# Row maxima of a grouped attention layer: weights taken as 128 adjacent queries instead of every fourth one, and the maxima brought to the queries' rows by a transpose and on-chip transfers

## The chip, the cores and the metric

The kernel runs on one core of one Trainium2 chip. The metric is the device time in microseconds of one execution of the program; lower is better. The profile of the kernel before is one execution taken by the hardware profiler. In its lines PE is the TensorE matmul, PEld the TensorE weight load, DVE is VectorE, ACT is ScalarE, POOL is GpSimd and SP is the engine that issues most DMAs.

## The reference, cut to what matters

Four cross-attention layers run one after the other on `x` (1 x 2048 x 256) with a context of 1601 keys (512 wide). Layers 1, 3 and 4 have 16 heads of width 64 and a bias on a few columns ("masked" layers in the kernel). The second layer, which the change concerns, has 16 query heads of width 16, of which four share one key and value head ("grouped"):

```python
xn = rmsnorm(x, norm_w)
q = (xn @ wq).reshape(B, T, N_HEADS, HEAD_DIM)
k = (cond @ wk).reshape(B, S, N_KV_HEADS, HEAD_DIM)
v = (cond @ wv).reshape(B, S, N_KV_HEADS, HEAD_DIM)
qg = q.reshape(B, T, N_KV_HEADS, n_rep, HEAD_DIM)
scores = jnp.einsum('btgrd,bsgd->bgrts', qg, k) * scale
attn = jax.nn.softmax(scores.astype(jnp.float32), axis=-1).astype(q.dtype)
out = jnp.einsum('bgrts,bsgd->btgrd', attn, v).reshape(B, T, N_HEADS * HEAD_DIM)
return residual + out @ wo
```

All of it is float32. The softmax subtracts each query's maximum over the keys, so that maximum has to be known before the exponentials are taken.

## The kernel before, in words

**Units.** Work is cut into units: one group of heads and one block of 512 queries. In the grouped layer a unit is four heads that share keys and values; each head has 16 rows of a 32-row quarter of the partitions (`QUARTERS`, rows 0, 32, 64 and 96). There are 4 groups and 4 query blocks, so 16 grouped units. `self.q` holds the unit's queries, features on the partitions and 512 queries along the free dimension; `self.u.kT` holds the keys in the same way.

**Steps.** A unit goes through 13 steps, one for each chunk of 128 keys (`TCH`), the last with 65. The loop at the end runs over steps in pairs. At one step three units are at work: one is scored (`scoring`), the one before it has its exponentials taken (`exping`, 18 steps after its own scoring step), and for that one, two steps later, the values are summed (`valuing`).

**One step of the grouped layer** (`Step.grouped`) consists of two parts, each for two scoring heads and the two other heads of the unit in `exping`. A part issues to TensorE, head by head in turn:

- `row_maxima` (L718): the queries are the weights and the keys stream, so that queries come out on the partitions and keys along the free dimension. It exists only for the maximum. Each step takes 128 of the queries and 512 keys; the last step takes the 65 remaining keys for all four sets of 128 queries. VectorE reduces each result (`row_maximum`, L731; L733 for the last step) into `row_top`.
- `scores_again` (L783): the keys are the weights and the queries stream; ScalarE takes the exponentials out of PSUM (`grouped_exp`, L795).
- then `values` (L813): the weights are the values and the exponentials stream, into `po`.

While only grouped units are at work the score results take six PSUM banks (`psum.singly`); in the built program each of the two kinds of score goes round three of them. A fourth result of a kind must wait until the first has been read.

**Which queries are the weights.** The weights of L718 are `self.q[r, columns(q)]`, and `columns(q)` is every fourth query:

```python
return slice(q, QB, QT)
```

So partition p of the result holds query 4p + q, and the 4 maxima of a partition are adjacent queries.

**From the maxima to the exponentials.** When a unit's scoring ends, `maxima` reduces `row_top` to `ntop` (L754, negated; 128 partitions x 4 heads x 4). `on_all_partitions` writes it to DRAM (L655) and reads it back, one row of 512 for each head (L658), into row 16 of the head's quarter of `self.q`. Row 16 of the keys is one, so that `scores_again` yields scores less their maximum. Nothing else is done with `ntop`.

**Order.** TensorE, ScalarE and VectorE run their instructions in the written order (the manual dependencies at the end). Between the steps stand pieces (`Pieces`): projections of queries (L576), keys and values of the next block (L440, L394, L546), denominators (L843, whose weights also use `columns(q)`), output projection (L862). A piece may be given a step at which it is due (`pieces.at`). One PSUM bank, `pm` in the pool `ps_m`, serves most of these pieces in turn.

Of the kernel before, what the change touches and what calls it, by code (L numbers as in the profile page):

```python
# [10 lines left out]
FP = mybir.dt.float32  # L11
# [7 lines left out]
P = 128  # L19
# [7 lines left out]
Piece = namedtuple("Piece", "run cost shared", defaults=(True,))  # L27
# [7 lines left out]
def tile_cross_attention_stack(ctx: ExitStack, tc: tile.TileContext, t: dict, out: bass.AP):  # L35
# [31 lines left out]
    nc = tc.nc  # L67
    x, cond = t["x"], t["ctx_2048"]
# [6 lines left out]
    QT = QB // P  # L75
# [13 lines left out]
    small = ctx.enter_context(tc.tile_pool(name="small", bufs=2))  # L89
    dram = ctx.enter_context(tc.tile_pool(name="dram", bufs=1, space=bass.MemoryType.DRAM))  # L90
    ps_o = ctx.enter_context(tc.tile_pool(name="ps_o", bufs=1, space=PSUM))
    ps_m = ctx.enter_context(tc.tile_pool(name="ps_m", bufs=1, space=PSUM))
    scores_pools = ctx.enter_context(ExitStack())

    ident = const.tile([P, P], FP, name="ident")
# [267 lines left out]
    QUARTERS = (0, 32, 64, 96)  # L363
# [107 lines left out]
    class Grouped:  # L471
# [5 lines left out]
        name = "L1_xattn_"  # L477
# [166 lines left out]
    def columns(q):  # L644


        return slice(q, QB, QT)

    def on_all_partitions(cols, to):


        n = cols.shape[1]
        rows = dram.tile([4, P, QT], FP, name="cols", bufs=4)[:n]
        with nc.allow_non_contiguous_dma(reason="1024 values, four at a time"):
            nc.sync.dma_start(out=rows.rearrange("h p q -> p h q"), in_=cols)  # L655
        for tile_, heads_ in to:
            src = rows[heads_].rearrange("(o h) p q -> o (h p q)", o=1)
            nc.sync.dma_start(out=tile_, in_=src.to_broadcast(tile_.shape))  # L658


    class Unit:
# [44 lines left out]
        def row_maxima(self, i, h, s):  # L706

            full = QT * (NK - 1)  # L710
            r = self.rows(h)
            if i < full:
                q, k = divmod(i, NK - 1)
                todo = [(q, *TBK[k], 0)]
            else:
                todo = [(q, TAIL, NTAIL, q * NTAIL) for q in range(QT)]
            for q, a, n, at in todo:
                nc.tensor.matmul(  # L718
                    s[:, at : at + n], self.q[r, columns(q)], self.u.kT[r, a : a + n],
                    start=True, stop=True,  # L720
                )
                yield
# [17 lines left out]
        def maxima(self):  # L740

            ntop = small.tile([P, len(self.pair), QT], FP, name="ntop")
            if self.masked:
                pt = psum.pair((2, QT, P))
                for h in range(2):
                    for q in range(QT):
                        nc.tensor.transpose(pt[:, h, q, :], self.top[:, h, columns(q)], ident)  # L747
                nc.vector.tensor_reduce(ntop, pt, AX.X, ALU.max, negate=True)  # L748
                self.spread = work.tile([P, 2, QB], FP, name="spread", bufs=1)
                on_all_partitions(  # L750
                    ntop, [(self.spread.rearrange("n h q -> n (h q)"), slice(0, 2))]
                )
            else:
                nc.vector.tensor_reduce(ntop, self.top, AX.X, ALU.max, negate=True)  # L754
                on_all_partitions(
                    ntop,
                    [(self.q[r + 16 : r + 17, :], slice(h, h + 1)) for h, r in enumerate(QUARTERS)],
                )

        def maxima_spread(self):  # L760
# [128 lines left out]
    for b in range(NB):  # L889
        nc.scalar.dma_start(  # L890
            out=x_rows[b], in_=x[0, ts(b, QB), :].rearrange("(n p) c -> p n c", p=P)
# [47 lines left out]
    def first_unit(i):  # L939

        if i < NT / 2:
            first_block(i)
        if i == 1:
            layers[0].load_wo(made[0, 0])
            for b in range(NB):
                keep(0, b)
                pieces.at(2 * i + 2 + 2 * b, [(0, biases[b])])
        if i == 3:
            token_marks(0)
        if i == 7:  # L950
            small_constants()
            for l in range(1, NL):
                token_marks(l)
            start_block(0)
# [59 lines left out]
    pieces = Pieces()  # L1014
# [127 lines left out]
    def masked(unit):  # L1142
        return unit and unit.masked

    for first in range(0, N + NT + DELAY + LAG + 16, 2):
        pair = [Step(first), Step(first + 1)]

        if any(masked(x.scoring) for x in pair):
            if psum.banks:
                psum.by_pairs()  # L1150
        elif pair[0].exping and not pair[0].exping.masked and not psum.banks:
            psum.singly()

        kn, cn = divmod(first + 2 - NT - DELAY, NT)
        ahead = of[kn] if cn == 0 and 0 <= kn < len(units) and of[kn].masked else None
        three = not ahead and not any(masked(x.exping) for x in pair)
        for x in pair:
            x.begin()
        for x in pair:
            if masked(x.exping):  # L1160
                if x.cb == 0 and x is pair[1]:
                    x.exping.maxima_spread()
                x.exping.subtract(x.cb)
        for x in pair:
            if masked(x.scoring):
                x.scoring.masked_scores(x.ca)

        ends = all(masked(x.valuing) for x in pair) and pair[0].cv == NT - 1
        if ends:
            pair[0].valuing.values(NT - 1)  # L1170
        for x in pair:
            if masked(x.exping):
                x.exping.masked_exp(x.cb)
        if ahead:
            ahead.maxima_spread()
        if not ends:
            for x in pair:
                if masked(x.valuing):
                    x.valuing.values(x.cv)
        first_unit(first // 2)  # L1180
        together = masked(pair[0].scoring) and (masked(pair[1].exping) or not pair[1].exping)
        for x in pair:
            x.grouped(three)
            x.end()
            if not together:
                pieces.steps([x.step], x.share())
        if together:
            pieces.pair([first, first + 1], round(pair[0].units_left() * NT / 2))
        if ends:
            pair[1].valuing.values(0)  # L1190
        for x in pair:
            if x.scoring and x.ca == NT - 1:
                x.scoring.maxima()


    last = {}
# [39 lines left out]
```

## Time and profile before

| what | value |
|---|---|
| time before, median of 3 runs | 4903.22 us (4901.65 to 4903.43) |
| the profiled execution: time; span | 4898.06 us; 4896.4 us |
| TensorE clock granted, mean | 0.981 |
| busy share: PE, PEld, DVE, ACT, POOL | 97%, 42%, 77%, 66%, 61% |
| grouped scoring alone (no grouped exponentials yet) | 1295 to 1385 us |
| grouped scoring and exponentials together | 1385 to 2266 us |

The busy share of PE says only that some matmul was in flight; matmuls overlap, and so a busy PE may still lose time to weight loads. The times of matmul ends are modelled by the profiler. The stages are found in the page's row of slices (the second layer is where GpSimd has nothing to do) and in the first and last starts of L718 and L783.

### The profile page before, as it was taken

How to read it: one execution, taken by the hardware profiler on the slowest of the kernel's cores; microseconds unless marked ns; L12 is line 12 of the kernel's file. 1: busy time of each engine (PE TensorE's matmuls, PEld its weight loads, DVE VectorE, ACT ScalarE, POOL GpSimd, SP SyncE). 2: the span in 40 equal slices, each digit the busy share in tenths (PEclk: the TensorE clock that was granted, in tenths of full speed). 3: DMA queues.
4: the chain of work that ended last, by engine and by line, in shares of the span. 5: the costliest groups of instructions: out<-in, count | busy, mean ns of one | idle time of the engine just before them, and what ended most of it. 6: DMA issues, size and time to landing. Idle time of an engine off the chain costs nothing.

```text
span 4896.4 us, 64042 instructions
## 1 busy us (share of the span) xinstructions
PE 4727.9 (97%) x24004; PEld 2059.7 (42%) x24004; DVE 3746.8 (77%) x3766; ACT 3221.9 (66%) x3994; POOL 2993.3 (61%) x1440
## 2 busy tenths in 40 slices
PE   8999999999999999999999999999999999999996
PEld 4444444443444444454344444444444444444432
DVE  5888888888766565653578888888888888888886
ACT  4777777777545544544567777777777777777774
POOL 3777777778610000000377777777777777777787
PEclk9999999999989999999899999999999999999998
DMA  4222222222210000011132222222232222222201
GB/s 146 87 83 78 87 75 88 80 80 73 65 38 21 20 21 20 19 41 45 44 92 88 83 80 82 77 88 77 78 90 79 83 78 87 75 88 84 76 29 35
DMA packets 354053, 337.87 MB, mean 69 GB/s; under 512 B 120681, under 2 KB 309353, under 8 KB 353744
## 3 DMA queue, kind: packets, MB, share of 16 engines
q1 hardware_dynamic: 350048, 328.41, 22.9%
q8 instruction: 189, 3.10, 0.3%
q0 software_dynamic: 1152, 3.28, 0.2%
q10 hardware_dynamic: 2544, 2.10, 0.1%
q14 instruction: 120, 0.98, 0.1%
HBM read 318.89 MB, written 14.82 MB: 68 GB/s over the span
## 4 chain that ended last, share of the span: by engine, by line
PE 87%; DVE 10%; issue 1%; POOL 1%; ACT 1%; DMA 0%; POOLq 0%; SPq 0%; DVEq 0%; ACTq 0%
PE po L813 28%; PE s L687 19%; PE t L718 8%; PE pm L394 7%; PE pm L440 6%; PE s L862 4%; PE pm L464 4%; PE t L783 3%; DVE ntop L748 2%; DVE rden L838 2%; PE s L834 2%; DVE xs L874 2%; PE s L747 2%; DVE top L704 1%; POOL sums L778 1%
## 5 line engine op out<-in xcount | busy, mean ns | idle before, releaser
L778 POOL TENSOR_TENSOR sums<-sums,p 128x1024 f32<-128x1024 f32 (+1 forms) x1152 | 2727.9, 2368 | 739.2 <-ACT p L773 568.3
L699 ACT COPY p<-s 128x1024 f32<-128x1024 f32 (+1 forms) x1248 | 1235.4, 1014 | 663.6 <-PE s L687 578.6
L813 PE MATMUL po<-p,v 128*64 128x512 f32 (+3 forms) x8320 | 1507.3, 529 | 8.9 <-ACT p L773 5.9
L768 DVE TENSOR_TENSOR p<-p,b 128x1024 f32<-128x1024 f32 (+1 forms) x1248 | 1461.3, 1209 | 55.2 <-ACT b L763 52.9
L704 DVE TENSOR_TENSOR top<-s,top 128x1024 f32<-128x1024 f32 (+1 forms) x1056 | 1291.2, 1223 | 239.1 <-ACT p L699 175.7
L687 PE MATMUL s<-q,kT 64*128 64x512 f32 (+1 forms) x4992 | 1342.2, 631 | 86.7 <-DVE ntop L748 23.7
L773 ACT ACTIVATE p<-p 128x1024 f32<-128x1024 f32 (+1 forms) x1248 | 1254.6, 1057 | 45.7 <-DVE p L768 44.3
L813 PEld LDWEIGHTS po<-p,v 128*64 128x64 f32 (+3 forms) x8320 | 367.0, 126 | 1096.5 <-issue 864.4
L687 PEld LDWEIGHTS s<-q,kT 64*128 64x128 f32 (+1 forms) x4992 | 390.0, 182 | 725.6 <-issue 218.7
L795 ACT ACTIVATE p<-t 128x512 f32<-128x512 f32 (+1 forms) x760 | 412.2, 594 | 410.8 <-PE t L718 373.8
L731 DVE TENSOR_REDUCE row_top<-t 128x1 f32<-128x512 f32 x700 | 451.2, 686 | 256.5 <-PE t L718 253.1
L854 POOL TENSOR_TENSOR oT<-oT,by 128x512 f32<-128x512 f32 x112 | 143.3, 1280 | 758.8 <-DMA by<-cols 365.6
L718 PE MATMUL t<-kT,q 32*128 32x512 f32 (+1 forms) x1880 | 560.5, 639 | 0.0
L783 PE MATMUL t<-q,kT 32*128 32x512 f32 (+1 forms) x1520 | 491.6, 659 | 0.0
L718 PEld LDWEIGHTS t<-kT,q 32*128 32x128 f32 x1880 | 295.4, 316 | 167.6 <-issue 83.3
L394 PEld LDWEIGHTS pm<-wv,ct 128*128 128x128 f32 (+1 forms) x2600 | 300.4, 187 | 130.3 <-issue 66.9
L394 PE MATMUL pm<-wv,ct 128*128 128x128 f32 (+2 forms) x2600 | 333.3, 281 | 2.2 <-ACT v L398 0.9
L440 PE MATMUL pm<-ct,wk 128*128 128x256 f32 (+1 forms) x1344 | 314.6, 377 | 2.7 <-issue 2.7
L440 PEld LDWEIGHTS pm<-ct,wk 128*128 128x128 f32 x1344 | 230.7, 190 | 157.9 <-issue 100.1
L748 DVE TENSOR_REDUCE ntop<-s 128x8 f32<-128x1024 f32 x96 | 117.6, 1225 | 232.7 <-PE s L747 232.7
L862 PE MATMUL s<-oT,wo 128*128 128x512 f32 x392 | 199.1, 631 | 16.2 <-POOL oT L854 12.5
L776 POOL COPY sums<-p 128x1024 f32<-128x1024 f32 x96 | 99.7, 1039 | 183.6 <-ACT p L773 183.6
(149 smaller groups left out, 2308.0 us busy)
## 6 DMA issues: line engine op xcount, KB each, us to landing
ct<-ctxT SPq DMA_DIRECT2D x288, 512.0 KB
xT<-xT SPq DMA_DIRECT2D x100, 512.0 KB
spread<-cols SPq DMA_DIRECT2D x96, 512.0 KB
by<-cols SPq DMA_DIRECT2D x192, 128.0 KB
xT<-xs SPq DMA_DIRECT2D x16, 512.0 KB
ct<-ctxT SPq DMA_DIRECT2D x48, 130.0 KB
wk<-in_L_xattn_Wk_dram SPq DMA_DIRECT2D x24, 256.0 KB
wv<-in_L_xattn_Wv_dram SPq DMA_DIRECT2D x24, 256.0 KB
```

What stands on the lines that cost most here:

```text
L394: nc.tensor.matmul(pv[:md, d, :f], ct(k)[:, d * P : d * P + md], wv[:, k, :], start=(k == 0), stop=(k == NCT - 1),)
L440: nc.tensor.matmul(pk, u.wk[:, k, :], ct(k), start=(k == 0), stop=(k == NCT - 1))
L687: nc.tensor.matmul(s[:m, h, :], self.u.kT[r, a : a + m], self.q[r, :], start=True, stop=(a != TAIL),)
L699: nc.scalar.copy(p[:m], s[:m])
L704: nc.vector.tensor_tensor(self.top[:m], s[:m], self.top[:m], ALU.max)
L718: nc.tensor.matmul(s[:, at : at + n], self.q[r, columns(q)], self.u.kT[r, a : a + n], start=True, stop=True,)
L731: nc.vector.tensor_reduce(self.top[:, of, q, k : k + 1], s, AX.X, ALU.max)
L768: nc.vector.tensor_tensor(self.p[c][:m], self.p[c][:m], self.less[:m], ALU.add)
L773: nc.scalar.activation(p[:m], p[:m], AF.Exp)
L778: nc.gpsimd.tensor_tensor(self.sums[:m], self.sums[:m], p[:m], ALU.add)
L783: nc.tensor.matmul(s[:m], self.u.kT[r, a : a + m], self.q[r, :], start=True, stop=True)
L813: nc.tensor.matmul(to, v, p, start=(c == 0 and not part), stop=(c == NT - 1 and part != 0))
```

## The change

The weights of L718 become 128 adjacent queries (`ts(q, P)`). Partition p of the result then holds query 128q + p. `maxima` only reduces to `ntop`; the way through DRAM is gone for this layer. A new piece, `maxima_rows`, is due two steps after the pair of steps that ended the scoring: TensorE transposes `ntop` (128 x 16) into `pm`, ScalarE copies the 16 rows of 128 to SBUF (`top_rows`), and four DMAs from SBUF to SBUF on SP's queue put each head's 4 rows of 128 side by side into row 16 of its quarter of `self.q`. The other uses of `columns(q)` and of `on_all_partitions` stay.

```diff
-                    s[:, at : at + n], self.q[r, columns(q)], self.u.kT[r, a : a + n],
+                    s[:, at : at + n], self.q[r, ts(q, P)], self.u.kT[r, a : a + n],
...
                 nc.vector.tensor_reduce(ntop, self.top, AX.X, ALU.max, negate=True)
-                on_all_partitions(
-                    ntop,
-                    [(self.q[r + 16 : r + 17, :], slice(h, h + 1)) for h, r in enumerate(QUARTERS)],
+                self.ntop = ntop
+
+        def maxima_rows(self):
+
+            n = 4 * QT
+            pt = ps_m.tile([P, P], FP, name="pm")
+            nc.tensor.transpose(pt[:n, :], self.ntop.rearrange("p h q -> p (h q)"), ident)
+            rows = small.tile([n, P], FP, name="top_rows", bufs=1)
+            nc.scalar.copy(rows, pt[:n, :])
+            for h, r in enumerate(QUARTERS):
+                nc.sync.dma_start(
+                    out=self.q[r + 16 : r + 17, :].rearrange("o (q p) -> o q p", p=P),
+                    in_=rows[h * QT : h * QT + QT, :],
                 )
...
                 x.scoring.maxima()
+                if not x.scoring.masked:
+                    pieces.at(first + 2, [(0, Piece(x.scoring.maxima_rows, 0.3))])
```

## The prediction

> **What bounds the kernel now.** I read the page first, for the stage; then the table of windows, the groups of instructions and the waits of that stage; last the timeline of a few steps.
>
> The change touches L718 alone, which runs from 1295 to 2266 us. The windows show the stage (us; busy time of PE, PEld, DVE, ACT, POOL; granted clock; DMA):
>
> ```profile
> 1295.00:1385.00 90.00, 76.45 (x280) 30.41 (x278) 65.03 (x62) 24.86 (x26) 42.13 (x19) 0.79 0.14 44
> 1385.00:2266.00 881.00, 881.00 (x6844) 434.90 (x6840) 510.83 (x836) 436.95 (x806) 25.92 (x36) 0.97 0.10 28
> ```
>
> For 881 us PE never rests, while DVE and ACT are busy 58% and 50%. So what PE's stream of loads and passes costs is what the stage costs. The groups of that stage show both kinds of score (busy, mean ns, idle before):
>
> ```profile
> L718 PEld LDWEIGHTS t<-kT,q 32*128 32x128 f32 x1878 | 295.2, 316 | 167.6 <-issue 83.3 <-DVE row_top L731 58.2 <-DVE row_top L733 11.8
> ...
> L783 PEld LDWEIGHTS t<-q,kT 32*128 32x128 f32 (+1 forms) x1520 | 161.3, 185 | 0.1
> ...
> L843 PEld LDWEIGHTS pm<-den_rows,oT 128*128 128x128 f32 x112 | 27.2, 327 | 5.8 <-issue 5.8
> ...
> L576 PEld LDWEIGHTS pm<-xT,wq 128*128 128x128 f32 x56 | 9.5, 189 | 12.5 <-issue 12.5
> ```
>
> The same 128 columns cost 316 and 327 ns where the weights are every fourth element (L718, L843), and 185 and 189 ns where they are adjacent (L783, L576). Is the difference on the path? The timeline of one part (start, duration), with two scoring heads and two exponential heads, each in two passes:
>
> ```profile
> 1700.38 0.81 PE L718 MATMUL t<-kT,q 32*128 32x512 f32 x1
> ...
> 1700.39 0.69 PE L783 MATMUL t<-q,kT 32*128 32x512 f32 x1
> ...
> 1701.04 0.60 PE L718 MATMUL t<-kT,q 32*128 32x512 f32 x2
> ...
> 1701.57 0.64 PE L813 MATMUL po<-p,v 128*32 128x256 f32 x8
> ...
> 1701.66 1.29 DVE L731 TENSOR_REDUCE row_top<-t 128x1 f32<-128x512 f32 x2 [0.48 <-PE t L718]
> ```
>
> and, after the last scoring, a part with the exponential heads alone:
>
> ```profile
> 2271.63 1.13 PE L783 MATMUL s<-q,kT 32*128 32x512 f32 x4
> 2272.68 0.64 PE L813 MATMUL po<-p,v 128*32 128x256 f32 x8
> ```
>
> L783's second passes are done 1.13 us after the start in both (in the first, at 1701.52). L718 takes 1.26 (1700.38 to 1701.64), and the values, which need all quarters, start at 1.19 instead of 1.05. The four quarters run side by side, and the slowest chain, L718's, sets the part.
>
> [...] L783's second load of a quarter begins 108 ns after the first (2271.624, 2271.732). [...] the trace gives 233 ns from load to load (1717.863, 1718.097). [...]
>
> **The change part by part.**
>
> *Ordinary parts.* A chain is load, pass, load, pass. The second load hides under the first pass[...]; the first stands open. So each part loses 233 - 108, measured between the two chains as 1.256 - 1.134 = 0.122 us. Half the parts take 1.19 us before their values and half 1.44: there the second L718 waits until the first reduce of the part before has emptied its bank (the 58.2 us above). A part's start to start is 1.756 or 2.014, and the latter ends with the reduce: chain 1.256, start 0.03, reduce 0.69, release 0.05. The chain is a term of both, so both fall by 0.122. I count 346 such parts between 1385 and 2266: 346 x 0.122 = **42.2**. Of them 24 run at half clock[...]: **2.9**.
>
> *Last steps.* With 65 keys a head issues four queries' sets, eight loads in a row:
>
> ```profile
> 1717.43 0.30 PEld L718 LDWEIGHTS t<-kT,q 32*128 32x128 f32 x1
> ...
> 1717.63 1.74 PEld L718 LDWEIGHTS t<-kT,q 32*128 32x128 f32 x14
> ...
> 1719.44 0.16 PEld L813 LDWEIGHTS po<-p,v 128*32 128x32 f32 x8
> ```
>
> The part takes 2.02 us to its values; eight loads at 0.233 are 1.86 of it. At 0.108, and with passes in order, so that the third cannot start before L783's second at 0.55, the last of the six remaining starts at 0.55 + 5 x 0.108 = 1.09 and ends 0.21 later: 1.30, less the 0.07 by which values start early, is 1.23. If loads run freely ahead it is L783's 1.05. 30 such parts x (2.02 - 1.23) = **23.7**; bounds 18 (loads of two quarters in each other's way) and 29.
>
> *Scoring alone (1295 to 1385).* DVE is busy 65 of 90 us, PE waits for its reduces, the clock is 0.79. Twelve steps gain at most a load each at half clock, and the last step: 6. At least 0. I take **3**.
>
> *Clock.* Ten-odd stretches of 3.4 us at half clock lie in the stage; some follow the slow last steps (1722, 1780, 1896). If those three go, about 1.2 us each; **3**, between -4 (new ones behind other pieces) and 12.
>
> *Added.* 16 transposes: one pass of 128 on a 16-column load. No row shows it alone; the pieces nearest are L834, 1.17 us for eight, and L546, 0.86 on average for two longer passes. So 0.15 to 0.86, and from below slightly less than nothing, because a pause lets the reduce empty the bank (0.26). I take 0.3 on 14 of them: **-4**, range -12 to +1. Each brings an ACT copy of 16 x 128 (a 128 x 256 copy takes 0.35; ACT is half idle, and only exponentials with a spare bank are behind it) and four SP issues (0.24 each, hidden: SP issues about a dozen transfers in a unit's 57 us). `pm` is used next in a later step, after that copy.
>
> *Removed and moved.* The write of 512 pieces to DRAM and four reads go; nothing waited for them, cost and gain nothing. The order of the changed program shows a few pieces (L546 above all) a step earlier or later, none added: nothing, because PE does them anyway.
>
> *Path of the maxima.* From transpose to the first L783 that reads the row lie 6 to 8 parts of about 1.74, 10 to 14 us. Needed: transpose 0.4, copy with an exponential ahead 0.9, four issues 1.0, one landing; DRAM's was 2.3 (L655 issued 1549.65 for 0.38, L658 at 1552.33). About 4.6: hidden. Only the landing from SBUF to SBUF is not shown in the trace; it is free up to some 7.5 us.
>
> Sum: 42.2 + 2.9 + 23.7 + 3 + 3 - 4 = 70.8, of the profiled execution's 4898.06: 4827.3. The median of the runs is 5.2 above that execution; so 4832.
>
> **Rivals.**
> - *The reduces keep the pace.* If the reduce's end is not tied to the chain, only the unhindered half of the parts shrinks and the wait of the other half grows: 173 x 0.122 = 21 instead of 42, and the last steps give 18; with the other terms 21 + 1 + 18 + 3 + 3 - 4 = 42: 4861. For it: 58.2 us of waiting for L731. Against: the reduce starts 0.03 us after the chain's end in every part that I looked at, and DVE is 58% busy.
> - *Late rows, slower.* [...] an L783 that waits for its row stops L718, values, everything. It needs more than the 10 us slack plus the 70.8 gained over 16 units (4.4 each), a landing above 12 us. A landing of 14 is 6.3 late, 1.9 of net loss a unit: 16 x 1.9 = 30, 4933. Against: three times 2.3 is still free; four descriptors of 512 bytes from four partitions to one are not shown before.
> - *Loads are not what it was.* If the step did not set the load's time, no gain but the cost: 4907. Against: L843 and L576 differ in it likewise.
>
> **How the numbers follow.** Main case 0.79, reduces' pace 0.13, late rows 0.05, no effect 0.02, other 0.01. Faster by over 0.2% (10 us, about what a measurement can tell): 0.93; within: 0.02; slower: 0.05. The main case's own bounds: best 42 + 3 + 29 + 6 + 12 + 1 = 93, 4810; worst 42 + 18 - 4 - 12 = 44, 4859. The range 4812 to 4860 takes in most of it and half of the first rival.
>
> **What would show it.** L718's loads at about 185 ns; the ordinary part at 1.07 and 1.32 before its values, in about equal number; last steps near 1.23; the stage from the first joint part to 2266 some 67 us shorter; no L783 waiting for a DMA; the other stages as before. Wrong it would be with loads still near 316, with longer waits for L731, or with `q` from `top_rows` as releaser.

## The result and the profile after

The changed kernel takes **4828.29 us** (median of 4 runs, 4821.27 to 4833.60) where the kernel before, on the same chip, takes 4902.43 (4 runs, 4901.25 to 4903.43). The ratio is **0.9848, interval 0.9833 to 0.9863**: faster by 1.5%, 74.1 us. The forecast was 4832.

In the file after the change the lines below L731 stand ten lower: L793 is what L783 was (exponential scores), L805 what L795 was, L823 what L813 was, L853 what L843 was. Each kernel of the experiments has its own line numbers too; the name of the tile tells which instruction is meant.

The two stages of the second layer in the windows of the changed kernel (us; busy time of PE, PEld, DVE, ACT, POOL; granted clock, DMA share, GB/s). The windows end where the corresponding work ends, so the first number is to be compared with 90 and 881 of before:

```profile
1288.80:1378.10 89.30, 75.61 (x281) 25.99 (x279) 64.89 (x62) 24.27 (x26) 41.59 (x19) 0.75 0.14 44
1378.10:2199.90 821.80, 821.02 (x6855) 330.02 (x6854) 510.79 (x835) 440.63 (x820) 25.86 (x36) 0.97 0.11 30
```

The joint stage (scoring and exponentials together) lost some 59 us, and in it the weight loads lost 105 us of busy time (434.9 to 330.0); DVE and ACT did what they did before. PE is still all but never idle (821.02 of 821.80), so the stage is still set by PE's stream. The scoring alone did not move. Counted from the start of the first joint part to the start of the last, as from here on, the stage went from 878.9 to 820.6 us, by 58.3.

The groups of that second window (busy us, mean ns of one | idle before, and what ended it):

```profile
L731 DVE TENSOR_REDUCE row_top<-t 128x1 f32<-128x512 f32 x700 | 451.2, 686 | 215.7 <-PE t L793 186.6 <-PE t L718 29.0
...
L718 PEld LDWEIGHTS t<-kT,q 32*128 32x128 f32 x1878 | 183.5, 187 | 161.0 <-issue 94.1 <-DVE row_top L731 54.0 <-DVE xs L884 8.3
L793 PEld LDWEIGHTS t<-q,kT 32*128 32x128 f32 (+1 forms) x1520 | 163.5, 184 | 4.3 <-ACT p L805 2.5 <-issue 1.0 <-ACT rms L616 0.5
```

L718's loads went from 316 to 187 ns, level with L793; L853, whose weights are still every fourth element, stays at 327. The reduces L731 used to be released by L718 and are now mostly put down to L793. A reduce reads L718's result alone; the profile names the pass that ended last before it, so this says only that the two chains now end together: the slower chain has become as short as the other. The 14 transposes of the stage keep PE busy for 3.8 us and their copies ACT for 3.4.

One pair of ordinary parts in the timeline of the changed kernel (start, duration):

```profile
1687.17 0.69 PE L718 MATMUL t<-kT,q 32*128 32x512 f32 x1
...
1688.33 1.29 DVE L731 TENSOR_REDUCE row_top<-t 128x1 f32<-128x512 f32 x2 [0.35 <-PE t L793]
...
1688.50 0.64 PE L823 MATMUL po<-p,v 128*32 128x256 f32 x8
...
1689.07 0.69 PE L718 MATMUL t<-kT,q 32*128 32x512 f32 x1
...
1690.14 0.64 PE L823 MATMUL po<-p,v 128*32 128x256 f32 x8
```

From a part's first pass to its values (L823): 1688.50 - 1687.17 = 1.33 and 1690.14 - 1689.07 = 1.07, where it was 1.44 and 1.19. Both kinds of part fell by about 0.12.

The two parts of a last step, the first that way and the second not:

```profile
1692.60 0.32 PE L718 MATMUL t<-kT,q 32*128 32x65 f32 x1
...
1693.67 0.64 PE L823 MATMUL po<-p,v 128*32 128x256 f32 x8
1693.76 1.08 ACT L805 ACTIVATE p<-t 128x512 f32<-128x512 f32 x2 [0.77 <-PE t L793]
...
1694.24 0.32 PE L718 MATMUL t<-kT,q 32*128 32x65 f32 x1
...
1694.90 0.18 PEld L793 LDWEIGHTS t<-q,kT 32*128 32x128 f32 x1 [0.20 <-ACT p L805]
...
1695.95 0.64 PE L823 MATMUL po<-p,v 128*32 128x256 f32 x8
```

The first takes 1.07 to its values, the second 1.71. The second's L793 load stands until 1694.90, and the line says for whom: the two exponentials of the part before, which started at 1693.76 and took 1.08, so they ended at 1694.84. Before the change the first part of a last step was 2.59 us long (1717.42 to 1720.01), and those exponentials were over by then.

### The profile page after: what moved, and what is told of

Its sections match the earlier page's. It is cut to its first block, busy times and chain, and to the rows that moved or that the text cites. A ratio compares the mean times of both kernels' runs of the same rounds, so it can differ in the third digit from the quotient of the medians.

```text
span 4828.2 us, 64072 instructions
## 1 busy us (share of the span) xinstructions
PE 4667.0 (97%) x24020; PEld 1949.9 (40%) x24020; DVE 3746.8 (78%) x3766; ACT 3225.1 (67%) x4010; POOL 2991.6 (62%) x1440
## 4 chain that ended last, share of the span: by engine, by line
PE 87%; DVE 10%; issue 1%; POOL 1%; ACT 1%; DMA 0%; POOLq 0%; ACTq 0%; DVEq 0%; SPq 0%
PE po L823 28%; PE s L687 20%; PE t L718 9%; PE pm L394 7%; PE pm L440 6%; PE s L872 4%; PE pm L464 4%; DVE ntop L748 2%; DVE rden L848 2%; PE s L844 2%; DVE xs L884 2%; PE s L747 2%; DVE top L704 1%; POOL sums L788 1%; PE t L793 1%
## 5 line engine op out<-in xcount | busy, mean ns | idle before, releaser
L823 PE MATMUL po<-p,v 128*64 128x512 f32 (+3 forms) x8320 | 1506.7, 528 | 8.8 <-ACT p L783 5.8
L783 ACT ACTIVATE p<-p 128x1024 f32<-128x1024 f32 (+1 forms) x1248 | 1254.8, 1057 | 49.1 <-DVE p L778 47.7
L823 PEld LDWEIGHTS po<-p,v 128*64 128x64 f32 (+3 forms) x8320 | 366.9, 126 | 1138.9 <-issue 905.4
L805 ACT ACTIVATE p<-t 128x512 f32<-128x512 f32 (+1 forms) x760 | 413.7, 594 | 337.3 <-PE t L793 300.5
L731 DVE TENSOR_REDUCE row_top<-t 128x1 f32<-128x512 f32 x700 | 451.2, 686 | 215.7 <-PE t L793 186.6
L793 PE MATMUL t<-q,kT 32*128 32x512 f32 (+1 forms) x1520 | 496.6, 656 | 0.0
L718 PE MATMUL t<-kT,q 32*128 32x512 f32 (+1 forms) x1880 | 490.1, 563 | 0.0
L718 PEld LDWEIGHTS t<-kT,q 32*128 32x128 f32 x1880 | 183.7, 187 | 161.0 <-issue 94.1
L872 PE MATMUL s<-oT,wo 128*128 128x512 f32 x392 | 199.1, 631 | 15.1 <-POOL oT L864 11.1
```

The lines of the kernel that those rows point to most:

```text
L718: nc.tensor.matmul(s[:, at : at + n], self.q[r, ts(q, P)], self.u.kT[r, a : a + n], start=True, stop=True,)
L731: nc.vector.tensor_reduce(self.top[:, of, q, k : k + 1], s, AX.X, ALU.max)
L783: nc.scalar.activation(p[:m], p[:m], AF.Exp)
L793: nc.tensor.matmul(s[:m], self.u.kT[r, a : a + m], self.q[r, :], start=True, stop=True)
L823: nc.tensor.matmul(to, v, p, start=(c == 0 and not part), stop=(c == NT - 1 and part != 0))
```

## The experiments

Each kernel is compared with runs of the kernel before on its own chip; those medians were 4908.4 to 4910.4, 6 to 8 us above the first chip's. The times expected below start from 4828, the first chip's, and so lie as much too low; the ratios and the stages are what to compare.

**The same two kernels again**, because the profiled pair holds two things that the change does not explain: some 8 us less in the first 43 us of the program, and a stage shorter by 58 instead of 67.

> The changed kernel once more, as the base for the others on the same chip: 4828, within 4821 to 4834. Its ordinary parts with 1.07 or 1.32 us before the values, last-step parts with 1.07 (first) and 1.71 (second).

> The kernel before once more, for a second trace: its stage from the first joint part to the last 879 us as in the first trace. Where the traces of before and after differ outside that stage (7.7 us in the first 43 us), theory: that is chance of the start, and before's second trace may have it or not; rival: the change moves it.

Measured: 4835.73 for the changed kernel, ratio 0.9851 (0.9835 to 0.9868); 4910.15 for the kernel before. In the second pair of traces an early pause (PE idle for 4.4 us until 31.9 us) stands in both kernels, and both reach the first L718 at 1296.8; so the 8 us were chance. The joint stage is 885.6 before, not the 879 expected, and 820.6 after: 65.0 less. What varies is the kernel before: it spent 54.6 us of the stage at half clock in the first trace and 68.3 in the second, the changed one 44.4 in both. The pairs give the parts of the gain twice over:

| us | first pair | second pair | forecast |
|---|---|---|---|
| 346 ordinary parts | -40.4 | -45.3 | -45.1 |
| 30 last-step parts | -21.1 | -22.2 | -23.7 |
| rest of the joint stage (transposes, other pieces) | +3.2 | +2.5 | +1 |
| joint stage | -58.3 | -65.0 | -67.8 |
| scoring alone | -0.5 | -2.5 | -3 |
| start of the program, and after the last L718 | -9.4 | -5.2 | 0 |
| profiled execution | -68.2 | -72.7 | -70.8 |

The last row but one is what remains of each difference of spans: in the first pair 7.0 of it lie ahead of the first L718, in the second nothing. The other 2.4 and 5.2 fall behind the last scoring part, where nothing was forecast; they are not explained. The forecast's 3 us for the clock are counted with the rest of the joint stage.

**One half of the change at a time.** Adjacent weights, with the maxima still going through DRAM:

```diff
-                    s[:, at : at + n], self.q[r, columns(q)], self.u.kT[r, a : a + n],
+                    s[:, at : at + n], self.q[r, ts(q, P)], self.u.kT[r, a : a + n],
...
+                rows_t = dram.tile([4, QT, P], FP, name="cols_t", bufs=4)
...
+                    nc.sync.dma_start(out=rows_t.rearrange("h q p -> p h q"), in_=ntop)
...
```

> Only the weights are changed (128 adjacent queries); the maxima still go through DRAM, written in single values so that the rows come out in order; no transpose. Theory (the weight loads are all of the gain): loads of L718 near 187 ns, ordinary parts 1.07 and 1.32, and 14 transposes of 0.2 us less than the changed kernel: 4825, within 4818 to 4832. Rival (leaving DRAM brings a good part of the gain): 4850 or more. Second rival (2048 single values make the write slow, and the first exponentials of a unit wait for their row): waits of L783 for a DMA, some us a unit.

The new way for the maxima, with every fourth query as weights (so that the rows hold the maxima of other queries):

```diff
-                    s[:, at : at + n], self.q[r, ts(q, P)], self.u.kT[r, a : a + n],
+                    s[:, at : at + n], self.q[r, columns(q)], self.u.kT[r, a : a + n],
```

> Only the path is changed: transpose, copy, transfers from SBUF to SBUF; the weights stay every fourth query, so each row gets the maxima of other queries. Theory: loads of L718 near 316 ns, parts 1.19 and 1.44 as before, and 16 transposes of 0.2 us more than before: 4906, within 4902 to 4910. Rival (the path brings part of the gain): 4890 or less.

Measured: the weights alone 4837.22, ratio 0.9849 (0.9831 to 0.9867), joint stage 819.5. The path alone 4900.36, ratio 0.9993 (0.9984 to 1.0001), joint stage 881.9. The group of L718's loads in each, weights alone first, then path alone:

```profile
L718 PEld LDWEIGHTS t<-kT,q 32*128 32x128 f32 x1880 | 183.1, 188 | 166.7 <-issue 96.2 <-DVE row_top L731 56.9 <-DVE xs L878 9.9
```

```profile
L718 PEld LDWEIGHTS t<-kT,q 32*128 32x128 f32 x1880 | 295.2, 316 | 164.1 <-issue 84.4 <-DVE row_top L731 54.8 <-DVE row_top L733 11.5
```

The load's time goes with the weights' step and with nothing else, and the whole gain goes with the load's time: the weights alone are as fast as the changed kernel on the same chip (4835.73), not 3 us faster as expected, a difference too small for these runs. The transpose and the four transfers neither gain nor cost anything that they can tell: the path alone has a median 8 us below the kernel before, but its runs spread from 4894 to 4912 and those of before from 4892 to 4913, and the joint stage lies between the two of before. No exponential score waited for a row in either trace: the maxima had time enough on either way.

**Does the cost grow with the step?** If every element costs by its distance, a step of two should lie between one and four (theory B); theory A takes it to load as a step of one does.

```diff
-                    s[:, at : at + n], self.q[r, columns(q)], self.u.kT[r, a : a + n],
+                    s[:, at : at + n], self.q[r, (q // 2) * 2 * P + q % 2 : (q // 2 + 1) * 2 * P : 2], self.u.kT[r, a : a + n],
```

> The weights are every second query (step of 8 bytes), the maxima go through DRAM in pairs of values. Theory A[...]: loads from load to load 0.108 to 0.112 as with adjacent queries, and the time of weights only, 4825. Theory B (the load grows with the step, half-way between 0.108 and 0.233): loads at about 0.15, each part 0.04 longer than with adjacent queries, 4845 to 4860.

Measured: 4831.02, ratio 0.9839 (0.9822 to 0.9855), joint stage 823.2. L718's loads in the joint stage of this kernel:

```profile
L718 PEld LDWEIGHTS t<-kT,q 32*128 32x128 f32 x1878 | 190.1, 195 | 167.1 <-issue 96.5 <-DVE row_top L731 57.1 <-DVE xs L882 9.9
```

195 ns against 187 at step one and 316 at step four; in the row of loads of a last step 0.117 us from load to load, against 0.112 and 0.233. So the cost does not go with the distance: a step of two costs 8 ns more than a step of one, a step of four 129. Why four costs so much more than two is not shown; no other step was tried.

**The second part of a last step.** The reading is that its second exponential head is given the bank that the second exponential of the part before still reads. If that is the wait, two rings of three banks, one for each kind of score, should free it: there the bank is that of the first exponential, which is over half a microsecond earlier.

```diff
-            self.banks = scores_pools.enter_context(tc.tile_pool(name="ps_t", bufs=6, space=PSUM))
+            self.banks = scores_pools.enter_context(tc.tile_pool(name="ps_t", bufs=3, space=PSUM))
+            self.own = scores_pools.enter_context(tc.tile_pool(name="ps_e", bufs=3, space=PSUM))
...
-                exps = psum.heads(three) if exping else []
+                exps = psum.heads(three, True) if exping else []
```

> The changed kernel with two pools of three banks, one for the scores of the maxima and one for those of the exponentials, instead of six from one pool. Theory (in the second part of the last step the second exponential head gets a bank whose reader is the second exponential of the part before): that part falls from 1.71 to about 1.27 before its values, fifteen times 0.44: the joint stage 820.6 becomes about 814. Rival (the exponentials themselves are late): 1.71 stays.

Measured: 4828.99, ratio 0.9836 (0.9819 to 0.9854). The second parts fall from 1.71 to 1.19 or 1.26, while six of the fifteen first parts rise from 1.07 to 1.32; the 30 last-step parts go from 58.9 to 53.3 us, the stage from 820.6 to 815.0, and no L793 of the stage waits for an exponential any more. So the wait came from how the six banks are shared. Which bank it was is inferred, no trace names it; but the description ahead of the prediction, that each kind of score goes round three of the six, can't hold in the last step, or two rings of three would have changed nothing. The whole program's interval overlaps that of the changed kernel; the gain is shown in the stage alone.

**Does the reduce set the pace?** Each L731 reduces only the first half of its 512 keys, so that it is shorter:

```diff
-                nc.vector.tensor_reduce(self.top[:, of, q, k : k + 1], s, AX.X, ALU.max)
+                nc.vector.tensor_reduce(self.top[:, of, q, k : k + 1], s[:, :, : QB // 2], AX.X, ALU.max)
```

> The changed kernel with the reduce L731 over 256 of the 512 columns; the maxima are then over part of the keys. Theory A (the reduce alone makes every other ordinary part 1.32 instead of 1.07): all are 1.07, 173 x 0.25 = 43 us off the joint stage, 778. Theory B (the wait for the exponential L805 lies just behind: its end is 1.16 + 0.60 + 0.05 = 1.81 after a part's start, the next part starts at 1.64): every other part is about 1.23, 173 x 0.09 = 15 us, 805. The last steps as before in both.

Measured: 4804.05, ratio 0.9789 (0.9771 to 0.9806). The group of the reduces in the joint stage, and the windows of the two stages:

```profile
L731 DVE TENSOR_REDUCE row_top<-t 128x1 f32<-128x256 f32 x693 | 262.1, 420 | 359.5 <-PE t L793 202.2 <-PE t L718 157.3
```

```profile
1288.80:1357.70 68.90, 60.04 (x314) 26.34 (x313) 44.52 (x58) 23.68 (x28) 40.60 (x21) 0.90 0.22 60
1357.70:2168.00 810.30, 808.21 (x6789) 313.87 (x6788) 327.65 (x837) 439.18 (x814) 30.69 (x38) 0.97 0.11 30
```

A reduce shorter by 266 ns takes 183 us off DVE's joint stage and only 10.3 off the stage, near theory B (15) and far from A (43). Over a third of the ordinary parts still take 1.20 or 1.26 us to their values instead of 1.07. One of them:

```profile
1679.79 0.59 ACT L805 ACTIVATE p<-t 128x512 f32<-128x512 f32 x1
...
1680.22 0.69 PE L718 MATMUL t<-kT,q 32*128 32x512 f32 x1
...
1680.43 0.69 PE L793 MATMUL t<-q,kT 32*128 32x512 f32 x1
...
1681.49 0.64 PE L823 MATMUL po<-p,v 128*32 128x256 f32 x8
```

Its second L793 head begins 0.2 late, just behind the end of the exponential (1680.38). So the chains of loads and passes set the pace where no bank is waited for; in the other parts the reduce holds the bank, and as soon as it is shorter the exponential does. In the stage of scoring alone the shorter reduce takes 20.5 off 89.4: that stage is the reduces', which is why faster loads brought it nothing.

**Are late rows as dear as feared?** The transposes come due three steps later, so that the rows arrive near or after their first reader:

```diff
-                    pieces.at(first + 2, [(0, Piece(x.scoring.maxima_rows, 0.3))])
+                    pieces.at(first + 5, [(0, Piece(x.scoring.maxima_rows, 0.3))])
```

> The changed kernel with the transpose of the maxima due five steps after the pair that ends the scoring, not two: between it and the first exponential score that needs the row lie none or two parts instead of six or eight. Theory (the path takes about 0.6 to the first issue, 0.6 for each further one and some 2 to land, and is hidden only by the parts between): eight units wait some 2 to 4 us each, the stage grows by 16 to 35 us, L793 waits for the transfers. Rival (the transfers land at once, or are not waited for): the stage stays at 821.

Measured: 4873.37, ratio 0.9930 (0.9912 to 0.9948), joint stage 854.4, 33.8 longer than in the changed kernel. A line of its waits (us in total, times, longest), and its timeline around one of them:

```profile
PE t L793 <- DMA q<-top_rows: 7.3, 7, 1.1
```

```profile
1505.94 0.28 PE L761 MATMUL pm<-ident,ntop 128*16 128x128 f32 x1
...
1506.15 1.12 PE L718 MATMUL t<-kT,q 32*128 32x512 f32 x2
...
1508.31 0.94 PE L793 MATMUL t<-q,kT 32*128 32x512 f32 x1 [1.04 <-DMA q<-top_rows]
...
1511.99 1.22 PE L718 MATMUL t<-kT,q 32*128 32x512 f32 x1
```

In seven units the first L793 starts 2.15 to 2.19 us after the part's first L718 (1508.31 and 1506.15), where both start together otherwise: 15.1 us in all. The 7.3 of the waits are only the ends of that, with PE idle, after the L718 passes already begun had run out. Behind six of the seven, 0 to 1.9 us after L793's start, a stretch of 3.4 or 6.8 us at half clock begins, in which passes take 1.22 instead of 0.69; behind the seventh, at 1621.7, there is none for 23 us. Half-clock time in the stage went from 44.4 to 78.5 us; by an estimate from these pass times half of the 34.1 added is lost, 17. With the 15.1 that makes 32 of the 33.8. A late row is dear by its wait and by the clock, in about equal shares.

**Adjacent everywhere.** Denominators, norm factors and the masked layers' transposes take every fourth element as weights too. First all of them, with the values written to DRAM one by one so that a row comes back in order:

```diff
-        return slice(q, QB, QT)
+        return ts(q, P)
...
-            nc.sync.dma_start(out=rows.rearrange("h p q -> p h q"), in_=cols)
+            nc.sync.dma_start(out=rows.rearrange("h q p -> p h q"), in_=cols)
```

> Adjacent queries at every use of columns(q), in all layers, and everything through DRAM as before, written in single values. Base: weights only, 4837. Theory: the 16 sets of grouped denominators have 8 loads at 0.245 that become 0.112, 13 to 15 us; the 4 sets of norm factors (3.83 each) become some 2, 7 us; the 191 sets of eight transposes of the masked layers (1.17 a set with every fourth, 1.04 a set where the first transposes of the context load adjacent columns) save 0.12 each, at most 23 us: 4837 - 14 - 7 - 20 = 4796, within 4788 to 4812. Rival A: the masked transposes are not what sets the pace there: 4816. Rival B (slower than weights only): 1024 single values land late, and the copies of the spread maxima wait for them: over 4840.

Then the same with the two rings:

> All adjacent, with two pools of three banks for the two kinds of score: 6 us less than all adjacent alone, some 4790. Second parts of the last step at 1.3 instead of 1.7; the joint stage near 800.

Measured: 5416.9, ratio 1.1044 (1.0994 to 1.1094), and 5412.35, ratio 1.1038 (1.0996 to 1.1079). Slower by a tenth: rival B's way, though far beyond the 4840 that it named. The joint grouped stage gained (819.5 with the weights alone, 807.8 here; a set of denominators takes 0.98 us instead of 1.96). The rings did not help here: second parts again took 1.26, but the stage was 815.2, not near 800; why is not settled. The masked layers lost the gain many times over. A line of the first kernel's waits (L763 copies the spread maxima, which the exponentials need):

```profile
ACT b L763 <- DMA spread<-cols: 530.3, 93, 10.0
```

and the way through DRAM on SP's queue, here and then in the kernel before:

```profile
629.27 0.62 SPq L655 DMA_DIRECT2D cols<-ntop  x1
...
640.38 0.34 SPq L658 DMA_DIRECT2D spread<-cols  x1
```

```profile
628.19 0.36 SPq L655 DMA_DIRECT2D cols<-ntop  x1
...
631.07 0.33 SPq L658 DMA_DIRECT2D spread<-cols  x1
```

In this pair 1024 values one by one take 11.1 us until the read back is issued, 256 pieces of 16 bytes 2.9. This kernel moves 198144 packets more than the kernel before (552197 and 354053), exactly the pieces added, and here four times the pieces take 3.9 times the time. In the masked layers the maximum is wanted at once: 93 waits of 5.7 us on average, 530 us in all beside the 507 by which the program is slower. In the weights-only kernel above the same kind of write cost nothing, because the grouped layer has the time.

**Only where there is time.** The changed kernel with two rings, and adjacent weights for the grouped layer's denominators and the norm factors; the masked layers as they were.

```diff
-                        pd[:, q, :], self.oT[:, columns(q)], den_rows, start=True, stop=True
+                        pd[:, q, :], self.oT[:, ts(q, P)], den_rows, start=True, stop=True
```

> The changed kernel with two pools of three banks, and adjacent queries also for the grouped layer's denominators and norm factors (written to DRAM in single values); the masked layers as they are. From two rings 4829: 16 sets of denominators at 0.98 instead of 1.96, 15.7 us; 4 sets of norm factors at 1.9 instead of 3.8, 7.7 us; fewer stretches at half clock behind them, some 5 us: 4800, within 4792 to 4812. What all adjacent lost, it lost in the masked layers, whose spread maxima waited for a 10 us write; if the grouped layer has that too, L854's product is late and the time is over 4830.

Measured: 4820.37, ratio 0.9816 (0.9794 to 0.9839). The denominators' loads and the joint stage of this kernel:

```profile
L855 PEld LDWEIGHTS pm<-den_rows,oT 128*128 128x128 f32 x112 | 13.6, 191 | 5.8 <-issue 5.8
```

```profile
1391.00:2190.00 799.00, 790.74 (x6860) 312.36 (x6855) 511.03 (x836) 439.61 (x819) 24.60 (x35) 0.99 0.11 30
```

327 became 191 ns, the joint stage from first part to last 797.3 (17.7 less than with the rings alone; some 28 were expected in all), half-clock time 17.1 us. And the program reaches its first L718 at 1302.5 instead of 1295.9, with the rings alone. So 20 us were missed. The norm factors are part of the cause: they too are now written in single values, and here somebody waits. From the chain that ended last, and the waits, ahead of the first L718:

```profile
1266.05 8.79 DMA factors<-rms
1274.85 3.59 DMA factor<-factors
```

```profile
DVE q L582 <- DMA factor<-factors: 7.8, 1, 7.8
```

With the rings alone the read back is issued 1.85 us after the write (1267.38, 1269.23) and DVE does not wait for it. Here DVE stands until 1278.5, PE then waits 3.4 us for DVE's next result where it waited 0.3, and two rows of passes behind it fall into half clock and take 1.6 and 1.4 us longer: 6.2 of the 6.6. In the joint stage DVE waits for such factors twice, 12.4 us. So "where there is time" held for the denominators and not for the factors. This kernel is the fastest complete version here, faster than the kernel before for certain; its interval and that of the changed kernel (0.9833 to 0.9863) overlap by a little.

## Why the prediction was right

The mechanism is shown: the open load of a part, 0.12 us shorter. That the sum came so close to the measured time is in part luck, as the terms show.

*Ordinary parts (right at full clock, wrong at half clock).* 45.1 forecast, 40.4 and 45.3 measured. Both kinds of part fell by 0.11 to 0.12, as argued from the chain being a term of both. That excludes the rival in which the reduces keep the pace: the part that waited fell too, and the gain is twice its 21. The halved reduces say less, for there the exponential takes the reduce's place.

The 2.9 for the 24 parts at half clock is the 0.122 once more for each: the author's estimate, with a load twice as long there. For every fourth element it is not. L718's loads of the joint stage before and after (shortest, median, longest in ns; half-clock stretches included):

```profile
L718 PEld LDWEIGHTS t<-kT,q x1880: 302/324/327, 1385.6 to 2266.1; 32*128 32x128 f32 x188
```

```profile
L718 PEld LDWEIGHTS t<-kT,q x1880: 181/184/333, 1378.1 to 2199.9; 32*128 32x128 f32 x188
```

Before, the loads that lie within half-clock stretches took 302 to 327 ns, as at full clock; after, they took 280 to 333 there, beside 181 to 187. So at half clock the step costs next to nothing: of the ordinary parts wholly inside such a stretch, seven of nine took 2.03 or 2.04 us to their values before, and five of seven 2.02 to 2.12 after. What made up for the missing term is the clock: ordinary parts held 44.7 and 55.9 us of half-clock time before and 37.4 after. If half of it is lost, the estimate from passes of 1.22 us instead of 0.69, 3.6 and 9.2 of the gain are the clock's, and the loads' share is 36 to 37, beside 42.2 forecast.

*Last steps (sum near by luck, premise wrong).* 23.7 forecast, 21.1 and 22.2 measured, by errors of opposite sign. The premise "with passes in order" fell: the recorded starts have L718's later passes going ahead of L793's second pass, which stands earlier in the program (eight L718 passes start from 1692.76 on ahead of L793's second at 1693.14, at least six of them of later matmuls), so the first part is 1.07 instead of 1.23. The written order, which the description ahead of the prediction gives TensorE, is thus not the order in which these passes start. And the second part meets a bank that was not counted: 1.71. The mean is 1.39, which from 2.02 gives 18.9. The rest comes from the kernel before: five and seven of its 30 parts took 2.14 to 2.28 instead of 2.02, and 2.6 and 4.0 us of them stood at half clock, against none after. What had been hidden by a slow part was late next, and the prediction did not look for it.

*Transposes (right, a little high).* 0.3 taken; about 0.21 of PE's time measured, from a transpose's start to the next pass (1505.94 and 1506.15 above): 2.9 us for 14. The rest of the joint stage is 3.2 and 2.5 longer.

*Clock and scoring alone (small, on the high side).* 3 and 3 forecast. The scoring alone gave 0.5 and 2.5, because it is bound by the reduces. The clock's part can't be told from chance: the kernel before varied by 13.7 us of half-clock time between two traces, while it and the changed kernel differ by 10.2 in the first pair. It lies within the other rows of the table.

*Path of the maxima (hidden, as argued; its terms were off).* The copy begins sooner than thought, the four issues are dearer than thought:

```profile
L765 SPq DMA_DIRECT2D q<-top_rows x64: 572/573/738, 1362.6 to 2209.9; - x64
```

0.573 us each, not 0.24. The fourth starts 2.53 us after the transpose, and a row is readable 1.77 after its issue (from the kernel with the later transposes: read 2.36 after the transpose, issued 0.59 after it): 4.3 in all, beside 4.6 forecast. No L793 waited for it. Three steps are six parts of about 1.74, 10.4 us; moved by that, the first reader was some 2.2 late, so about 8 us of slack are left in the changed kernel.

*Late rows (rival, excluded here).* It is real once the rows are late: 2.2 us late in seven units takes back nearly half of the gain.

*The base.* The first profiled execution of before lies low among its runs, as was said, and the addition of 5.2 to the sum was right. The remaining 3.7 of 4832 is inside what the runs scatter.

## What to carry to other kernels

Look at the element step of a matmul's weights: for these fp32 loads at full clock, every second element loaded nearly as fast as adjacent ones (195 and 187 ns a load), every fourth at half the rate (0.233 us from load to load instead of 0.112). Before moving the values into another order to get there, ask who waits for them and how many pieces the transfer becomes; where nobody waited it was free, where the masked layers' exponentials waited it cost a tenth of the program. And when one slow stretch is removed, look for the buffer that its length was covering.

## What the runs showed of the hardware that was not expected

- A load of weights took 195 ns at step two, 187 at step one, 316 at step four: not in proportion to the step.
- L718's loads at step four did not slow down with PE's clock (302 to 327 ns at full and at half clock); the adjacent ones did (181 to 187, and 280 to 333).
- The masked layers' transposes with every fourth element as weights had loads of 209 ns on average, not 316, and 142 when adjacent: the same step cost less there. Why was not tried.
- With the later transposes PE was idle for 1.03 to 1.07 us and half clock followed at six places of seven. Nor is idle time all: the joint stage of the kernel before, where PE was busy for all of its 881 us, had 54.6 us at half clock. What brings these stretches on is not shown.
- A transfer of four rows of 512 bytes from SBUF to SBUF holds SP for 0.573 us at its issue, a row read from DRAM for 0.24.
